# Moving four small transfers of a convolution layer from SyncE's queue to GpSimd's and ScalarE's

## The chip, the cores and the metric

The kernel runs on one core of one Trainium2 chip. The metric is the device time of one launch in microseconds (us). The kernel before took 3350.49 us, the median of three runs (3349.91 to 3353.61). A separate, profiled execution gives the durations used below.

A core has five engines, each with an instruction queue of its own that is worked through in order: PE (matrix products), DVE (VectorE), ACT (ScalarE), POOL (GpSimd) and SP (SyncE, which here only issues transfers). A transfer between the main memory and the on-chip memory is issued by one of SP, ACT or POOL and carried out by 16 DMA engines. An instruction that needs data waits for a semaphore; while it waits, nothing behind it on the same queue starts.

## What is computed

Four layers follow each other on one image of 256 x 256 pixels with 128 channels; each normalises the image by groups of channels and adds what it computes to it. The first three (an attention, and two triangle multiplications) are not touched by the change. The fourth is a convolution layer, in the reference:

```python
def c1(t):        # 3 x 3 convolution from 128 channels to one
    return conv(t, w1, SAME) + b1
def c2(t):        # 128 x 128 product at each pixel
    return einsum('bhwc,cd->bhwd', t, w2c) + b2
t = relu(c1(x))
y = concatenate([x[:, :1], x[:, 1:] + t[:, :-1]], axis=1)
u = relu(c1(y))
z_main = u + roll(y, 1, axis=1)
z = concatenate([z_main[:, :H-2], u[:, H-1:H] + y[:, H-2:H-1], y[:, H-1:H]], axis=1)
v = relu(c2(z))
p = concatenate([z[:, :, :1], z[:, :, 1:] + v[:, :, :-1]], axis=2)
r = relu(c2(p))
q_main = r + roll(p, 1, axis=2)
q = concatenate([q_main[:, :, :W-2], r[:, :, W-1:W] + p[:, :, W-2:W-1], p[:, :, W-1:W]], axis=2)
```

t and u have one channel: they are images of 256 x 256 numbers, made from the 3 x 3 convolution and added to all 128 channels.

## The kernel before

The convolution layer works on groups of 8 image rows (R = 8): 32 groups, with the 128 channels on the 128 partitions and 2048 pixels along each. The one-channel images are worked on in blocks of 16 rows (BR = 16), each spread over all 128 partitions with 33 numbers on each; there are 16 blocks, so one block belongs to two groups. The order of the instructions on each engine is the order in which the program writes them (a manual schedule), so the loop at L1695 is the order of all queues.

A block's way through the machine is this:

- `load9` (L1459) loads a group of the image x, 1 MB, eight groups ahead, from SP's queue.
- `taps` (L1464) forms, six groups ahead, the nine products of the 3 x 3 filter on PE; ACT copies them out (L1472), and SP stores them (L1477, four stores).
- `load_block` (L1494) loads them back shifted, in the block's layout (L1487).
- `sum_taps` (L1503, DVE) adds nine taps; `relu_t` (L1515, ACT) and `shift_t` (L1519 and L1522, POOL) give the block of t.
- `keep_t` (L1526) stores this block of t to the buffer tD, one row lower; `load_t` (L1529) loads the block's rows from tD, which shifts t by one image row.
- `image_u` (L1536, DVE) and `relu_u` (L1540, ACT) give u; `image_e` (L1545, POOL) adds the shifted t to u, which gives e, all that is to be added to the channels.
- `keep_e` (L1547) stores e to the buffer eD; `load_e` (L1561) loads the two groups of it as one long row each into the tile `er`, in two transfers.
- `spread_e` (L1572, POOL) copies such a row to all 128 partitions, into a tile that has one buffer.
- `start_z` (L1580, ACT) writes the scaled x into PSUM, and `finish_z` (L1595, DVE) adds the spread e: z.
- `p_half` and `q_half` (L1609, L1623, L1626 on DVE, products L1601 on PE), `residual` (L1615 to L1617, POOL) and the copy L1710 on ACT form p and q; `emit` (L1631) transposes q on PE (L1638), ACT copies it out (L1639), SP stores 1 MB (L1640).

The two-buffer PSUM pool `p9psX` is shared by `start_z`, `taps` and the transposes, in turn: two tiles of z, one of taps, two of transposes. So a transpose waits for the copy L1472 or for finish_z, and the next group's start_z waits for L1639.

For the block b = s // 2 + 2, t is made in the even group s, and u and e in the odd group that follows. In the kernel before, all of keep_t, load_t, keep_e and load_e are issued by SP, and at the head of the next group: keep_t and load_t in the odd group after load9, keep_e and load_e in the even group before load9. A load waits on SP until its store has landed. Blocks 0 to 2 are made ahead of this (`begin_image`, L1671, and `end_image`, L1678, in groups 0 and 1).

Of the kernel before, what the change touches and what calls it, by code (L numbers as in the profile page):

```python
# [16 lines left out]
P = 128  # L17
N = 256
# [14 lines left out]
def kernel(ctx: ExitStack, tc: tile.TileContext, a: dict, out: bass.AP):  # L33
    nc = tc.nc
# [33 lines left out]
    tD = dram.tile([1, (N + 2) * NP], F32, name="tD")  # L68
    eD = dram.tile([1, N * NP], F32, name="eD")
# [1031 lines left out]
    with tc.tile_pool(name="x5", bufs=7) as x5_pool, tc.tile_pool(name="p5", bufs=2) as sb, tc.tile_pool(  # L1101
# [95 lines left out]
        for s in range(NSC):  # L1197
            b, j = divmod(s, KB)
# [246 lines left out]
    NR = N // R  # L1445
    H = R // 2
    BR = 16
    NB = N // BR
    BW = NP // 8
    LEAD = 6  # L1450
    with tc.tile_pool(name="p9", bufs=2) as sb, tc.tile_pool(name="p9psM", bufs=2, space=PSUM) as psM, tc.tile_pool(
# [3 lines left out]
        xs, zs, pbs, qs, blocks = {}, {}, {}, {}, {}  # L1455
# [3 lines left out]
        def load9(s):  # L1459
            if s < NR:  # L1460
                xs[s] = sb.tile([P, R, N], F32, name="p9_x", bufs=9)
                nc.sync.dma_start(xs[s], x3r[:, s * R : (s + 1) * R, :])
# [37 lines left out]
        def image_rows(d, row, n=BR):  # L1500
            return d[:, row * NP : (row + n) * NP].rearrange("o (p w) -> p (o w)", w=BW)
# [15 lines left out]
        def shift_t(b):  # L1517
            k = blocks[b]
            nc.gpsimd.tensor_tensor(k["t"], k["t"], inside, ALU.mult)  # L1519
            t = k["t"][:, 0:BW]  # L1520
            nine = bass.AP(tensor=t.tensor, offset=t.offset, ap=[list(t.ap[0]), [1, BW], [1, TAPS]])
            nc.gpsimd.tensor_tensor(  # L1522
                k["prod"][:, :, 0:TAPS], nine, wsum.unsqueeze(1).to_broadcast([P, BW, TAPS]), ALU.mult
            )

        def keep_t(b):  # L1526
            nc.sync.dma_start(image_rows(tD, b * BR + 1), blocks[b]["t"][:, 4 : 4 + BW])

        def load_t(b):  # L1529
            t2 = blocks[b]["t2"] = sb.tile([P, BW], F32, name="p9_t2")  # L1530
            nc.sync.dma_start(t2, image_rows(tD, b * BR))

        def image_u(b):
            k = blocks[b]
# [3 lines left out]
        def relu_u(b):  # L1538
            k = blocks[b]
            nc.scalar.activation(k["u"], k["u"], AF.Relu, bias=b1)  # L1540

        def image_e(b):
            k = blocks[b]
            k["e"] = sb.tile([P, BW], F32, name="p9_e")
            nc.gpsimd.tensor_tensor(k["e"], k["u"], k["t2"], ALU.add)  # L1545

        def keep_e(b):  # L1547
            k = blocks.pop(b)
            e = k["e"]
            if b < NB - 1:  # L1550
                nc.sync.dma_start(image_rows(eD, b * BR), e)
            else:
                nc.sync.dma_start(image_rows(eD, N - BR, BR - 2), e[0 : P - 16, :])
                nc.sync.dma_start(image_rows(eD, N - 2, 1), e[P - 8 : P, :])
                nc.sync.dma_start(image_rows(eD, N - 1, 1), k["t"][P - 8 : P, 4 : 4 + BW])

        def row_e(s):
            at = 32 * (s % 4)
            return er[at : at + 1, :]

        def load_e(b):  # L1561

            for s in range(2 * b, 2 * b + 2):
                nc.sync.dma_start(
                    row_e(s).rearrange("o (h w) -> o h w", w=N),
                    eD.rearrange("o (h w) -> o h w", w=NP)[:, s * R : (s + 1) * R, 4 : 4 + N],
                )

        def spread_e(s):
            if s < NR:  # L1570
                ebs[s] = sb.tile([P, SC], F32, name="p9_eb", bufs=1)
                nc.gpsimd.partition_broadcast(ebs[s], row_e(s))  # L1572

        def start_z(s):

            zps[s] = [psX.tile([P, H, N], F32, name="p9_zp", tag="x") for _ in range(2)]

            def take(lo, hi, src):
                h = lo // H
                nc.scalar.activation(zps[s][h][:, lo - h * H : hi - h * H, :], src, AF.Identity, bias=k0, scale=r3)  # L1580

            take(0, 1, xs[s - 1][:, R - 1 : R, :] if s else xe[:, 1:2, :])
            take(1, H, xs[s][:, 0 : H - 1, :])
            if s + 1 < NR:
                take(H, R, xs[s][:, H - 1 : R - 1, :])
            else:
                take(H, R - 2, xs[s][:, H - 1 : R - 3, :])
                take(R - 2, R, xs[s][:, R - 2 : R, :])

        def finish_z(s):  # L1590
            zs[s] = sb.tile([P, R, N], F32, name="p9_z", bufs=3)
            zf, eb = zs[s].rearrange("p h w -> p (h w)"), ebs.pop(s)
            for h, zp in enumerate(zps.pop(s)):
                hs = slice(h * H2, (h + 1) * H2)
                nc.vector.tensor_tensor(zf[:, hs], zp.rearrange("p h w -> p (h w)"), eb[:, hs], ALU.add)  # L1595

        def product9(src, h):
            pm = psM.tile([P, H, N], F32, name="p9_pm")
            for c in range(2):
                r = h * H + 2 * c  # L1600
                nc.tensor.matmul(  # L1601
                    pm[:, 2 * c : 2 * c + 2, :], lhsT=w2c, rhs=src[:, r : r + 2, :], start=True, stop=True
                )
            return pm

        def p_half(s, h):
            rows_ = slice(h * H, (h + 1) * H)
            pm = product9(zs[s], h)
            nc.vector.scalar_tensor_tensor(  # L1609
                pbs[s][:, rows_, 1:N], pm[:, :, 0 : N - 1], kcol[:, 0:1], zs[s][:, rows_, 1:N], ALU.max, ALU.add  # L1610
            )
# [7 lines left out]
        def q_half(s, h):  # L1619
            rows_ = slice(h * H, (h + 1) * H)  # L1620
            q = qs[s]
            pm = product9(pbs[s], h)
            nc.vector.scalar_tensor_tensor(  # L1623
                q[:, rows_, 0 : N - 2], pm[:, :, 0 : N - 2], kcol[:, 1:2], q[:, rows_, 0 : N - 2], ALU.max, ALU.add
            )
            nc.vector.scalar_tensor_tensor(  # L1626
                q[:, rows_, N - 2 : N - 1], pm[:, :, N - 1 : N], kcol[:, 1:2], q[:, rows_, N - 2 : N - 1],
                ALU.max, ALU.add,
            )
# [41 lines left out]
        def begin_image(b):  # L1671
            sum_taps(b)
            relu_t(b)
            shift_t(b)
            keep_t(b)
            load_t(b)

        def end_image(b):  # L1678
            image_u(b)
            relu_u(b)  # L1680
            image_e(b)
            keep_e(b)
            load_e(b)
# [10 lines left out]
        spread_e(1)  # L1694
        for s in range(NR + 2):  # L1695
            b = s // 2 + 2
            if s > 3 and s % 2 == 0 and b <= NB:
                keep_e(b - 1)
                load_e(b - 1)
            load9(s + 8)  # L1700
            if s > 1 and s % 2 == 1 and b < NB:
                keep_t(b)
                load_t(b)
            if s < NR:
                pbs[s] = sb.tile([P, R, N], F32, name="p9_pb")
                nc.scalar.activation(pbs[s][:, :, 0:1], zs[s][:, :, 0:1], AF.Identity, bias=kcol[:, 0:1])
                if s + 1 < NR:
                    start_z(s + 1)
                qs[s] = sb.tile([P, R, N], F32, name="p9_q", bufs=3)
                nc.scalar.activation(qs[s], xs[s], AF.Identity, bias=kcol[:, 2:3])  # L1710
                p_half(s, 0)
                p_half(s, 1)
                del xs[s]
            if s < 2:
                begin_image(s + 1)
            if s + 1 < NR:
                finish_z(s + 1)
            if s < 2:
                end_image(s + 1)
            if 0 < s <= NR:  # L1720
                q_half(s - 1, 0)
                q_half(s - 1, 1)
                del pbs[s - 1], zs[s - 1]
            if s < NR:
                residual(s)
                spread_e(s + 2)
            if s < 2:

                for i in range(2):
                    taps(xs[4 + 2 * s + i], (4 + 2 * s + i) * R, 4)  # L1730
                load_block(s + 2)
            elif b < NB:
                sum_taps(b) if s % 2 == 0 else image_u(b)
            if s > 1 and s + LEAD < NR:
                taps(xs[s + LEAD], (s + LEAD) * R, 4)
            if s > 1 and s % 2 == 1 and b + 1 < NB:
                load_block(b + 1)
            if s > 1:
                emit(s - 2)
                if b < NB:  # L1740
                    if s % 2 == 0:
                        relu_t(b)
                        shift_t(b)
                    else:
                        relu_u(b)
                        image_e(b)
            if 0 < s <= NR:
                last = qs[s - 1][:, :, N - 1 : N]
                nc.scalar.activation(last, last, AF.Identity, bias=kcol[:, 1:2])
# [182 lines left out]
```

## Time and profile before

| what | us |
|---|---|
| median of three runs | 3350.49 |
| the profiled execution | 3354.71 |
| its span | 3353.0 |
| convolution layer, from group 0's L1710 to the end | 2960 to 3353 |
| group 2's L1710 to group 26's | 3001.08 to 3287.06 |
| L1472 (copy of the taps), each | 0.69 |
| L1710, each | 1.99 |
| L1615 (the large part of residual), each | 4.52 |
| L1572 (spread_e), each | 2.29 |
| L1639, each | 1.01 |

Engine times in the profile are those of the instruction itself. For a transfer that SP or ACT issues, the line (SPq, ACTq) is the time in which the queue was occupied with issuing it, not the transfer; when it has landed shows only in who starts next. For transfers of GpSimd the profile gives the time to landing as well. "Idle before" names what the engine waited for. L numbers are lines of the kernel before.

### The profile page before, as it was taken

To read this page: it belongs to the slowest core of one execution; us is meant where nothing else is said; L and a number is where in the kernel's file an instruction comes from. 1 tells how busy PE (TensorE), PEld (TensorE's weight loads), DVE (VectorE), ACT (ScalarE), POOL (GpSimd) and SP (SyncE) were. 2 spreads that over 40 slices of the span, in tenths; PEclk is the share of its full clock that TensorE was granted. 3 is DMA by queue.
4 is the path that set the end of the run, shared out by engine and by line. 5 is a ranking of instruction groups with operands and counts; after the bars stand their busy time and mean duration, and the time that the engine had idled before them with its cause. 6 is when DMAs were issued, how large, how long until landed. Compare 5 with 4: busy or idle time off the path is not lost. (4 is left out here: it accounts for less than half of the span.)

```text
span 3353.0 us, 51718 instructions
## 1 busy us (share of the span) xinstructions
PE 3050.1 (91%) x19780; PEld 1631.7 (49%) x19780; DVE 2243.0 (67%) x2532; ACT 2039.4 (61%) x2274; POOL 1753.9 (52%) x984
## 2 busy tenths in 40 slices
PE   5669999999999999967996999999999999749888
PEld 4515555555555555532532444444899533214444
DVE  5627888888888888863555545444555688647666
ACT  3567777777777777734586544543444477636666
POOL 4055777777777777730384000000555588546666
PEclk8889999999999999988997999999999999879999
DMA  9983333333333333359598676865999899746665
GB/s 355 370 313 94 109 120 111 111 119 109 121 107 118 108 121 109 121 209 375 171 384 343 256 270 248 305 233 216 351 350 350 319 389 384 312 137 190 194 191 148
DMA packets 298035, 749.46 MB, mean 224 GB/s; under 512 B 74679, under 2 KB 145289, under 8 KB 248601
## 3 DMA queue, kind: packets, MB, share of 16 engines
q1 hardware_dynamic: 289847, 735.49, 61.3%
q0 software_dynamic: 7648, 9.55, 0.8%
q8 instruction: 159, 2.61, 0.3%
q10 hardware_dynamic: 288, 1.05, 0.1%
q14 instruction: 93, 0.76, 0.1%
HBM read 458.34 MB, written 287.64 MB: 222 GB/s over the span
## 5 line engine op out<-in xcount | busy, mean ns | idle before, releaser
L565 DVE TENSOR_TENSOR p_e<-p_S,triT 128x1024 f32<-128x1024 f32 x512 | 609.3, 1212 | 144.2 <-PE p_S L555 144.2
L575 POOL TENSOR_TENSOR p_es<-p_e 128x1024 f32<-128x1024 f32 x256 | 603.4, 2368 | 123.8 <-issue 65.2
L573 ACT ACTIVATE p_e<-p_e,mbT 128x1024 f32<-128x1024 f32 x512 | 552.0, 1138 | 59.8 <-DVE p_e L565 59.6
L1172 PE MATMUL p_pm<-p_zn,wf 128*128 128x512 f32 x1040 | 449.3, 593 | 2.3 <-ACT p_a L1207 1.9
L540 PE MATMUL p_mm<-p_xn,w 128*128 128x512 f32 x768 | 404.6, 610 | 0.3 <-DVE p_v L535 0.3
L1172 PEld LDWEIGHTS p_pm<-p_zn,wf 128*128 128x128 f32 x1040 | 196.6, 190 | 255.1 <-issue 246.5
L555 PE MATMUL p_S<-p_q,p_k 32*128 32x256 f32 x4096 | 294.9, 400 | 3.5 <-DVE p_e L565 3.3
L1262 POOL MEMSET k<- 128x512 f32 x1 | 0.5, 520 | 505.8 <-DVE p_zn L1165 505.8
L555 PEld LDWEIGHTS p_S<-p_q,p_k 32*128 32x128 f32 x4096 | 185.7, 184 | 159.5 <-PE p_mm L531 91.7
L514 POOL TENSOR_TENSOR p_xn<-p_xn,p_rs 128x1024 f32<-128x1024 f32 x63 | 151.1, 2398 | 205.1 <-DMA p_rb<-rzD 129.1
L1890 PE MATMUL tp_z<-p_B,tp_at 128*128 128x256 f32 x1024 | 250.5, 388 | 0.7 <-DMA p_B<-bD 0.5
L588 PE MATMUL p_o<-p_e,p_v 128*32 128x256 f32 x4096 | 247.6, 382 | 0.0
L1293 POOL TENSOR_TENSOR k<-k,p_sq 128x512 f32<-128x512 f32 x128 | 163.0, 1273 | 159.1 <-ACT p_sq L1291 159.1
L1890 PEld LDWEIGHTS tp_z<-p_B,tp_at 128*128 128x128 f32 x1024 | 185.1, 191 | 23.2 <-DVE tp_at L1881 1.5
L540 PEld LDWEIGHTS p_mm<-p_xn,w 128*128 128x128 f32 x768 | 125.6, 190 | 104.2 <-issue 87.9
L1292 DVE TENSOR_TENSOR k<-tp_z,k 128x512 f32<-128x512 f32 x128 | 88.5, 692 | 126.8 <-ACT p_sq L1291 126.8
L588 PEld LDWEIGHTS p_o<-p_e,p_v 128*32 128x32 f32 x4096 | 120.0, 109 | 109.3 <-ACT p_g L546 41.5
L1289 ACT COPY p_K<-tp_z 128x512 f32<-128x512 f32 x128 | 75.1, 586 | 157.5 <-PE tp_z L1890 157.5
L546 ACT ACTIVATE p_g<-p_mm,bgh 128x512 f32<-128x512 f32 x128 | 88.0, 687 | 131.2 <-PE p_mm L540 131.2
L544 ACT ACTIVATE p_k<-p_mm,cqkg 128x512 f32<-128x512 f32 x128 | 88.1, 689 | 125.1 <-PE p_mm L540 124.9
L531 PEld LDWEIGHTS p_mm<-w,p_xn 128*128 128x128 f32 x1024 | 134.4, 191 | 61.1 <-issue 60.4
L1211 DVE SCALAR_TENSOR_TENSOR p_b<-p_pm,b2w,p_b 128x1024 f32<-128x1024 f32 x64 | 82.1, 1283 | 118.4 <-PE p_pm L1172 104.0
(374 smaller groups left out, 6092.3 us busy)
## 6 DMA issues: line engine op xcount, KB each, us to landing
p_x<-x2T SPq DMA_DIRECT2D x60, 1024.0 KB
x<-x1T SPq DMA_DIRECT2D x51, 1024.0 KB
p_x<-in_x_dram SPq DMA_DIRECT2D x32, 1024.0 KB
p_x<-xT SPq DMA_DIRECT2D x64, 512.0 KB
x2T<-x SPq DMA_DIRECT2D x32, 1024.0 KB
aD<-p_a SPq DMA_DIRECT2D x32, 1024.0 KB
bD<-p_b SPq DMA_DIRECT2D x32, 1024.0 KB
p_A<-aD SPq DMA_DIRECT2D x32, 1024.0 KB
```

The lines of the kernel that those rows point to most:

```text
L514: nc.gpsimd.tensor_tensor(xn, xn, groups[g]["rs"], ALU.mult)
L531: nc.tensor.matmul(pm[:, k * D : (k + 1) * D], lhsT=t["xn"][:, b * P : (b + 1) * P], rhs=wf[:, 2 * D : 3 * D], start=True, stop=True,)
L540: nc.tensor.matmul(pm, lhsT=w, rhs=t["xn"][:, cs_], start=True, stop=True)
L555: nc.tensor.matmul(Ss[h // 2][:, h % 2, u, :], lhsT=t["k"][hp, r * N + u * P : r * N + (u + 1) * P], rhs=t["q"][hp, r * N : (r + 1) * N], ...
L565: nc.vector.tensor_tensor(e[:, :, 2 * p : 2 * p + 2, :].rearrange("p u h n -> p h u n"), Ss[p], triT[:, 2 * p : 2 * p + 2, :, :], ALU.add,)
L573: nc.scalar.activation(e[:, u, :, :], e[:, u, :, :], AF.Exp, bias=mbT[:, u, i : i + 1])
L575: nc.gpsimd.tensor_tensor(es, e[:, 0, :, :], e[:, 1, :, :], ALU.add)
L588: nc.tensor.matmul(t["o"][hp, r % 2, :], lhsT=t["v"][:, r * 2 + u, hp], rhs=e[:, u, h, :], start=(u == 0), stop=(u == 1),)
L1172: nc.tensor.matmul(pm[:, c, :], lhsT=wf2[:, i, :], rhs=zns[s][:, k * CK : (k + 1) * CK], start=True, stop=True)
L1292: nc.vector.tensor_tensor(k1, pz, k1, ALU.add)
L1293: nc.gpsimd.tensor_tensor(k2, k2, sq, ALU.add)
L1890: nc.tensor.matmul(pz[:, t, :], lhsT=at[:, u, t * P : (t + 1) * P], rhs=Bc[:, u, :], start=(u == 0), stop=(u == 1))
```

## The change

The helpers get a parameter for the queue that issues them, with SP as default, which groups 0 and 1 keep. In the loop keep_t moves behind shift_t, and keep_e behind image_e, each on GpSimd's queue; so both are issued in the group in which the block is made. load_e (two transfers, even groups) and load_t (one, odd groups) move to ScalarE's queue, behind the copy L1710 of the group in whose head SP issued them before. In the last block keep_e is three stores. The amounts, addresses and numbers of transfers are the same.

```diff
-        def keep_t(b):
-            nc.sync.dma_start(image_rows(tD, b * BR + 1), blocks[b]["t"][:, 4 : 4 + BW])
-
-        def load_t(b):
+        def keep_t(b, queue=nc.sync):
+            queue.dma_start(image_rows(tD, b * BR + 1), blocks[b]["t"][:, 4 : 4 + BW])
+
+        def load_t(b, queue=nc.sync):
             t2 = blocks[b]["t2"] = sb.tile([P, BW], F32, name="p9_t2")
-            nc.sync.dma_start(t2, image_rows(tD, b * BR))
+            queue.dma_start(t2, image_rows(tD, b * BR))
...
-        def keep_e(b):
+        def keep_e(b, queue=nc.sync):
             k = blocks.pop(b)
             e = k["e"]
             if b < NB - 1:
-                nc.sync.dma_start(image_rows(eD, b * BR), e)
+                queue.dma_start(image_rows(eD, b * BR), e)
...
-        def load_e(b):
+        def load_e(b, queue=nc.sync):
 
             for s in range(2 * b, 2 * b + 2):
-                nc.sync.dma_start(
+                queue.dma_start(
                     row_e(s).rearrange("o (h w) -> o h w", w=N),
...
         for s in range(NR + 2):
             b = s // 2 + 2
-            if s > 3 and s % 2 == 0 and b <= NB:
-                keep_e(b - 1)
-                load_e(b - 1)
             load9(s + 8)
-            if s > 1 and s % 2 == 1 and b < NB:
-                keep_t(b)
-                load_t(b)
             if s < NR:
...
                 nc.scalar.activation(qs[s], xs[s], AF.Identity, bias=kcol[:, 2:3])
+            if s > 3 and s % 2 == 0 and b <= NB:
+                load_e(b - 1, nc.scalar)
+            if s > 1 and s % 2 == 1 and b < NB:
+                load_t(b, nc.scalar)
+            if s < NR:
                 p_half(s, 0)
                 p_half(s, 1)
...
                     if s % 2 == 0:
                         relu_t(b)
                         shift_t(b)
+                        keep_t(b, nc.gpsimd)
                     else:
                         relu_u(b)
                         image_e(b)
+                        keep_e(b, nc.gpsimd)
```

More of the change, by code (lines that the diff above doesn't have):

```diff
@@ L1550, in keep_e @@
             if b < NB - 1:
-                nc.sync.dma_start(image_rows(eD, b * BR), e)
+                queue.dma_start(image_rows(eD, b * BR), e)
             else:
-                nc.sync.dma_start(image_rows(eD, N - BR, BR - 2), e[0 : P - 16, :])
-                nc.sync.dma_start(image_rows(eD, N - 2, 1), e[P - 8 : P, :])
-                nc.sync.dma_start(image_rows(eD, N - 1, 1), k["t"][P - 8 : P, 4 : 4 + BW])
+                queue.dma_start(image_rows(eD, N - BR, BR - 2), e[0 : P - 16, :])
+                queue.dma_start(image_rows(eD, N - 2, 1), e[P - 8 : P, :])
+                queue.dma_start(image_rows(eD, N - 1, 1), k["t"][P - 8 : P, 4 : 4 + BW])
         def row_e(s):
```

## The prediction

> **What bounds the kernel now.** I read the table of 40 slices to find the last stage, then the start of each group of the convolution layer (ScalarE's L1710 runs once in each of its 32 groups), then the busy time in windows, the waits of each engine, and the timeline of one pair of groups.
>
> L1710 starts at 3023.37, 3033.14 and 3042.95 us in groups 4, 5, 6: 9.8 us a group. From group 7 on it alternates, 3078.69, 3092.82, 3102.74: 14.1 and 9.9. From group 2 (3001.08) to group 26 (3287.06) twelve pairs take 286.0 us, 23.8 a pair, where two undisturbed groups take 19.6. The columns below are the window, its length, each engine's busy time (and instructions), PE clock, DMA share and GB/s:
> ```profile
> 3000.00:3050.00 50.00, 48.66 (x200) 23.77 (x199) 40.83 (x47) 36.75 (x46) 40.21 (x27) 1.00 0.64 179
> 3150.00:3200.00 50.00, 43.58 (x164) 21.64 (x163) 34.98 (x40) 32.33 (x43) 31.26 (x22) 0.93 0.69 198
> ```
> In the first window PE is full (48.7 of 50); in the second nothing is, so a latency bounds it. The waits of POOL, DVE, PE and SP between 3000 and 3290 us (total, times, longest) name it:
> ```profile
> POOL p_eb L1572 <- DMA p_er<-eD: 47.1, 9, 6.5
> POOL p_e L1545 <- DMA p_t<-tD: 21.8, 8, 3.0
> DVE p_z L1595 <- POOL p_eb L1572: 42.0, 12, 5.2
> PE p_pp L1468 <- DVE p_z L1595: 30.8, 11, 3.9
> SPq L1531 <- DMA tD<-p_t: 62.0, 12, 5.9
> SPq L1564 <- DMA eD<-p_e: 29.5, 11, 3.5
> ```
> PE waits for z, z for the spread e, the spread for e's rows from memory. The timeline of POOL and of SP's queue closes the ring:
> ```profile
> 3080.55 2.29 POOL L1572 PARTITION_BROADCAST p_eb<-p_er  x1 [4.66 <-DMA p_er<-eD]
> 3082.92 0.27 POOL L1519 TENSOR_TENSOR p_t<-p_t,p_in 128x41 f32<-128x41 f32 x1
> 3083.27 0.81 POOL L1522 TENSOR_TENSOR p_prod<-p_t,wsum 128x297 f32<-128x297 f32 x1
> ...
> 3094.13 0.26 POOL L1545 TENSOR_TENSOR p_e<-p_u,p_t 128x33 f32<-128x33 f32 x1 [2.84 <-DMA p_t<-tD]
> ...
> 3104.68 2.29 POOL L1572 PARTITION_BROADCAST p_eb<-p_er  x1 [4.91 <-DMA p_er<-eD]
> ```
> ```profile
> 3082.11 3.86 SPq L1462 DMA_DIRECT2D p_x<-x3T  x1
> 3086.06 0.42 SPq L1527 DMA_DIRECT2D tD<-p_t  x1
> 3092.31 0.32 SPq L1531 DMA_DIRECT2D p_t<-tD  x1
> ...
> 3096.51 0.98 SPq L1640 DMA_DIRECT2D out_dram<-p_o  x1
> 3097.59 2.56 SPq L1551 DMA_DIRECT2D eD<-p_e  x1
> 3102.48 1.27 SPq L1564 DMA_DIRECT2D p_er<-eD  x2
> ```
> Read down: spread and shift_t to 3084.08 (3.53); SP still issues an image load, so the store of t starts 1.98 later; it lands and the load is let go at 3092.31 (6.25); t is back at 3094.13 (1.82); e made (0.26); SP reaches its store 3.20 later; landed at 3102.48 (4.89); rows loaded by 3104.68 (2.20). Sum 24.13, the whole period. POOL, DVE and PE only follow.
>
> [...] a store behind large transfers on SP's queue needs 4.9 to 6.3 us. [...] after a PE gap of 2.85 us the window 3084 to 3086 has clock 0.50, and the tap products take 1.93 instead of 1.07 us, the transposes 2.54 instead of 1.97: 1.4 us.
>
> **The change, part by part**, in microseconds per pair (even group E, odd group O); st is the start of ScalarE's L1472 of a group.
>
> *SP.* It loses five issues and the two waits on stores (62.0 + 29.5 us above). SP is not on the path otherwise; its gain is that output stores and image loads are issued up to a group earlier: 3096.51 above stores what ScalarE had ready at 3089.65. Worth nothing in itself, but it moves the 2 MB of each group to just behind the copies of L1639.
>
> *POOL, keep_t and keep_e.* Two issues a pair. GpSimd's stores to triD (rows below) cost 0.51 each, so 1.0 a pair. POOL's work is then 2 x (4.9 + 2.4) + 1.2 + 0.3 + 1.0 = 17.1, under 19.6: free as long as 2.5 of slack remain. The 1.98 and 3.20 of SP's lateness vanish.
>
> *The landing, called L*, from the start of POOL's issue to release. This is the unknown. GpSimd's stores to triD in the first layer (min/median/max in ns, then us) bound it:
> ```profile
> L424 POOL DMA_DIRECT2D triD<-p_tr x93: 502/508/538, 163.7 to 243.5; - x93
> DMA to landing us min/median/max: 1.8/6.0/8.0
> ```
> Asked window by window: 1.8 with the DMA engines nearly idle (share 0.05), 3.0 at 0.11, 3.9 at 0.60, 5.0 to 6.5 at 0.8 to 1.0, at most 8.0. A store of t starts (below) 6.9 after st of E, and the group's 2 MB, at 334 to 393 GB/s over some 5.7 us, are sent from about 3.5 to 10 after st: in the middle. The store of e comes at about 4 after a delayed st of O, at the start of the next burst. I take L = 4.8 for both, between 3.9 and 5.5; ends 1.8 and 8.0.
>
> *ACT, load_t and load_e.* They stand behind L1710 and in front of L1472, L1639, relu and start_z of the next group. Each waits for its store, and ACT's queue waits with it. Issue costs 0.32 for t and 1.27 for the two rows of e (SP's rows). The pause of ACT between L1710 and L1472 is 1.69, so the cover is thin. When the loads are let go:
> - L1710 of E ends 1.69 before st(E). residual 4.89 and 0.07 of gap, spread 2.29 + 0.1, shift_t 1.17 + 0.1 follow on POOL: store of t at st(E) + 6.9. st(O) is free at 6.9 + L + 0.32 = 12.0, instead of 9.8. So ACT, and with it the second half of the transposes on PE (it needs L1472's buffer), stand for 2.2.
> - relu_u comes 3.3 after st(O), image_e then, so the store of e at 15.8; the load is done at 15.8 + 4.8 + 1.3 = 21.9. Without this wait the next st(E) comes 9.8 after st(O), at 21.8: covered.
> - PE's gap of 2.2 is shorter than the 2.85 that halved the clock: I add 0.6, between 0 and 1.4.
>
> Period: 6.9 + 4.8 + 0.32 + 9.8 + 0.6 = 22.4. A second ring, L1472 to the end of the next L1710 (8.1) and then POOL's 8.5, gives 16.6 + 4.8 + 0.4 = 21.8: below it. Rows of e arrive 0.93 after their issue, before residual of E ends, so the 4.9 of POOL's wait is gone.
>
> *Order.* The instruction lists of both kernels show nothing else moved: the stores stand right behind L1522 and L1545 on POOL, the loads right behind L1710 on ACT; PE and DVE are as before.
>
> **Sum.** Twelve pairs: 286.0 - 12 x 22.4 = 17 saved. Groups 26 to 28 run at 18.4 the pair, with no tap products; the last load waits there cost about 1. Gain 16. The profiled execution took 3354.7 (span 3353.0 and 1.7 around it) and would take 3338.7; the median of the runs is 4.2 lower, 3350.5, so the time is 3334.
>
> **Rivals.**
> - *Fast: [...].* L about 3.0, as at light load. Period 6.9 + 3.0 + 0.3 + 9.8 = 20.0 (PE again sets it at 19.6 if L is under 2.6). 12 x 3.8 = 46 less 1: 3306. [...] Against: triD's landings [...] needed 5 to 6.5 in busy stretches. Chance 0.28.
> - *Nothing:* L of 5.5 to 6.1 gives 23.4 to 24.3, against 23.8 now: 3350. Chance 0.10.
> - *Slower: ACT stands behind its own load.* The place is the load of t in front of L1472. At L = 6.8, as in the worst busy stretches, st(O) comes at 14.0, PE idles 4.2 and pays the clock's 1.3: 25.1 a pair, 15 lost, 1 at the end: 3366. It decides from L = 5.9 (6.9 + 5.9 + 0.3 + 9.8 + 1.0 = 23.9). Against: DMA share in these windows is 0.62 to 0.70, with lulls of 0.1 to 0.2. Chance 0.25.
> - *The change does not do what it says:* excluded by the lists.
>
> **Chances.** Forecast 0.37, fast 0.28, nothing 0.10, slower 0.25. About 0.2% (6.7 us) is what a measurement of this kernel can tell from no change. Faster 0.65, same 0.10, slower 0.25. Range 3306 to 3362: L from 3.0 to about 6.5, with less than a tenth left out on each side. The forecast alone: L 3.6 to 5.5, 3314 to 3345.
>
> **What would show it.** Right: POOL's wait for eD's rows falls from 47 to a few us; ACT waits in front of L1472 for DMA tD<-p_t about 2 a pair; L1710 spacing near 12 then 10; GpSimd's stores 0.5 each and landing in 4 to 5.5. Wrong: no wait of ACT on tD, and groups at 9.8 (the fast rival); or PE idle over 4 in odd groups with clock 0.50 (the slow one); or a new wait elsewhere, for instance POOL late by more than its slack of 2.5, or image_e waiting for t again.

## The result, and the profile after

The changed kernel takes 3345.54 us (median of 10 runs, 3340.94 to 3349.4). In the same comparison the kernel before took 3355.23 (10 runs, 3349.91 to 3359.84). The ratio is 0.997, with an interval of 0.996 to 0.998: 9.7 us less. The forecast was 16 us less than the profiled execution of the kernel before, and a time of 3334. The profiled execution of the changed kernel took 3345.7 (span 3342.8). The copy into q, L1710 before, is L1704 now; the lines up to L1640 have kept their numbers.

The waits of ScalarE, of PE and of POOL between 2990 and 3280 us (total, times, longest) are these:
```profile
ACT p_st L1472 <- DMA tD<-p_t: 42.7, 11, 4.7
ACT p_st L1472 <- PE p_pp L1468: 30.4, 15, 3.4
```
```profile
PE p_pt L1638 <- ACT p_st L1472: 22.2, 11, 2.8
```
```profile
POOL p_q L1615 <- ACT p_q L1704: 48.9, 22, 3.8
...
POOL p_eb L1572 <- DMA p_er<-eD: 0.7, 1, 0.7
```
POOL's wait for the rows of e, 47.1 before, is all but gone. In its place stands ScalarE, in front of L1472, until the store of t has landed: 11 times, 3.9 each. Of each 3.9 about 1.7 is the pause that ScalarE has there in an undisturbed group (the other waits at L1472, 30.4 in 15, are 2.0 each); the other 2.2 are the price of issuing the load from ScalarE. PE hands the wait on: its second half of the transposes waits 22.2 / 11 = 2.0 for L1472. POOL now waits for ScalarE (48.9), as a follower.

The tile views of tD and of eD give GpSimd's stores and the time to landing:
```profile
L1527 POOL DMA_DIRECT2D tD<-p_t x13: 555/555/582, 3018.7 to 3285.3; - x13
...
DMA to landing us min/median/max: 2.3/5.0/6.1
```
```profile
L1551 POOL DMA_DIRECT2D eD<-p_e x12: 555/555/577, 3029.9 to 3275.2; - x12
...
DMA to landing us min/median/max: 1.5/3.0/4.4
```
One pair of groups on the timeline shows the new ring, the cycle of waits that sets the period. The columns are start, duration, engine, line, operation, and in brackets the idle time before it with its cause:
```profile
3058.25 0.69 ACT L1472 ACTIVATE p_st<-p_pp,s 128x512 f32<-128x512 f32 x1 [1.73 <-PE p_pp L1468]
...
3064.83 0.56 POOL L1527 DMA_DIRECT2D tD<-p_t  x1
...
3069.88 0.32 ACTq L1531 DMA_DIRECT2D p_t<-tD  x1
3070.38 0.69 ACT L1472 ACTIVATE p_st<-p_pp,s 128x512 f32<-128x512 f32 x1 [4.04 <-DMA tD<-p_t]
...
3071.12 1.09 PE L1638 MATMUL p_pt<-ident,p_q 128*128 128x128 f32 x8 [2.14 <-ACT p_st L1472]
...
3074.31 0.56 POOL L1551 DMA_DIRECT2D eD<-p_e  x1 [0.29 <-POOL p_e L1545]
...
3077.35 1.95 ACTq L1564 DMA_DIRECT2D p_er<-eD  x2
...
3080.15 0.69 ACT L1472 ACTIVATE p_st<-p_pp,s 128x512 f32<-128x512 f32 x1 [1.73 <-PE p_pp L1468]
```
Read down from L1472 of the even group: the store of t 6.58 later, landed and the load issued 5.05 after that, L1472 of the odd group 12.13 after the first, the next even one 9.77 on. The pair takes 21.9. Twelve pairs, from group 2's copy into q to group 26's, take 267.55 (285.98 before): 22.3 a pair.

### The profile page after: what moved, and what is told of

Same layout as the page of the kernel before. It is cut to its first block, busy times and chain, and to the rows that moved or that the text cites. A ratio compares the mean times of both kernels' runs of the same rounds, so it can differ in the third digit from the quotient of the medians.

```text
span 3342.8 us, 51721 instructions
## 1 busy us (share of the span) xinstructions
PE 3049.3 (91%) x19780; PEld 1630.5 (49%) x19780; DVE 2241.1 (67%) x2532; ACT 2038.4 (61%) x2274; POOL 1769.9 (53%) x1012
## 5 line engine op out<-in xcount | busy, mean ns | idle before, releaser
L1615 POOL TENSOR_TENSOR p_q<-p_q,p_pb 128x2024 f32<-128x2024 f32 x32 | 144.1, 4504 | 64.8 <-ACT p_q L1704 52.8
```

Source lines behind the costliest of these rows:

```text
L1615: nc.gpsimd.tensor_tensor(q[:, :, 1 : N - 2], q[:, :, 1 : N - 2], pb[:, :, 0 : N - 3], ALU.add)
```

## The experiments

The theory: in every pair ScalarE's queue is held by its own load of t, for as long as the store needs to land, and this sets the period. Rival one: the wait for e's rows, or POOL's own work, still sets it, and ScalarE only follows. Rival two: the time is one of loaded DMA engines, and who issues a transfer doesn't matter. The table has the medians and, from one profile each, the layer (group 0's copy into q to the end) and the mean of the twelve pairs from group 2's copy into q to group 26's.

| kernel | median us (runs) | ratio to before | layer | pair |
|---|---|---|---|---|
| before, first profile | 3355.23 (10) | 1 | 392.7 | 23.83 |
| after, first profile | 3345.54 (10) | 0.997 [0.996, 0.998] | 375.5 | 22.30 |
| n1_before | 3353.94 (12) | 1.0002 [0.9994, 1.0011] | 391.9 | 23.92 |
| n2_after | 3341.19 (5) | 0.9964 [0.995, 0.9978] | 378.2 | 22.61 |
| e3_loads_sp | 3323.60 (4) | 0.9918 [0.9901, 0.9934] | 363.4 | 21.42 |
| e4_load_t_late | 3346.53 (8) | 0.9976 [0.9965, 0.9987] | 387.8 | 23.42 |
| e5_stores_sp | 3367.87 (5) | 1.0042 [1.0028, 1.0056] | 406.0 | 24.89 |
| e6_no_out | 3335.90 (4) | 0.995 [0.9933, 0.9966] | 375.0 | 22.46 |
| e7_loads_first | 3320.14 (4) | 0.9902 [0.9886, 0.9919] | 359.7 | 21.14 |
| e8_both_late | 3326.96 (4) | 0.9919 [0.9903, 0.9936] | 362.1 | 21.24 |

The kernel before took 3353.92 beside the first four experiments and 3353.93 beside the last four.

### n1_before and n2_after: both kernels again

No edit. The first profile after had the layer begin 7 us later than the one before (2967.31 against 2960.34), which no part of the change explains.

> The kernel before, unchanged, profiled again beside the others of this call. What is asked: whether the stages ahead of the convolution layer take the same time in each profile. In the first two profiles the convolution layer (from its first L1710 or L1704 to the end) took 392.7 us before and 375.5 after, 17.2 less, but its first L1710 came 7.0 us later in the profile after, so the spans differ by 10.2 only. Theory (the change touches the layer alone; the 7 us are from chip to chip and run to run): ahead of the layer this profile and the one of the changed kernel in this call agree within 2 us, the layer takes 391 to 394, and the changed kernel is 15 to 18 us faster than this one here. Rival (the change costs something ahead of the layer): the first L1710 at 2960 here and 2967 for the changed kernel again.

> The changed kernel, unchanged, profiled again on the same chip as the kernel before. Theory: the layer takes 374 to 377 us, 22.3 us for a pair of groups, the first L1704 comes where the first L1710 of the kernel before does within 2 us, and the kernel is 15 to 18 us faster. Rival: the first L1704 comes 7 us later than the other's L1710, and 10 us are gained.

The layer began at 2963.74 in n1_before and at 2960.98 in n2_after: the 7 us did not come again, so they belong to that execution (a shift of an us or two is not excluded by two profiles each). The layer's saving shows again, 391.9 - 378.2 = 13.7, and on average 392.3 - 376.9 = 15.4. Timed, it is 3353.92 - 3341.19 = 12.7 here and 9.7 in the first comparison, less than the 15 to 18 expected.

The waits are not quite those of the first profile: ScalarE stood for t in 8 odd groups here, 31.9 us in all between 2990 and 3290, and once for the load of e:
```profile
3051.99 1.28 ACTq L1564 DMA_DIRECT2D p_er<-eD  x2
3053.48 0.69 ACT L1472 ACTIVATE p_st<-p_pp,s 128x512 f32<-128x512 f32 x1 [5.45 <-issue]
```
In the odd group ahead of it, t had held next to nothing: its L1472 waited 1.94, for PE. The step from group 6 to group 7 took 14.4 in place of 9.8. e4 and e6 come back to this.

### e3_loads_sp: the loads back on SyncE, the stores left with GpSimd

```diff
-                load_e(b - 1, nc.scalar)
+                load_e(b - 1)
...
-                load_t(b, nc.scalar)
+                load_t(b)
```

> The stores stay on GpSimd, the loads of t and e go back to SP's queue, at the same place in the program (behind load9). Theory, that what is left over the 19.6 us of PE for a pair is ScalarE standing in front of L1472 behind its own load: the wait of L1472 for tD is gone, groups of 9.8 to 10.2, a pair 19.6 to 20.4 instead of 22.3, and the kernel is 22 to 32 us faster than the changed kernel, about 40 faster than the one before. Rival, that the landing of GpSimd's store itself sets the period, whoever waits for it: a pair stays at 22 to 22.5 and the time within 4 us of the changed kernel. A third: SP stands instead, and its stores of taps and output come late; then DVE waits for L1487, and a pair is 21 to 24.

Both loads stand behind load9 here, where the kernel before had load_e ahead of it; e7 has them ahead. Measured 3323.6: 30 us under the kernel before and 17.6 under n2_after, less than the 22 to 32 expected, at 21.4 a pair for 19.6 to 20.4. From group 4 on most steps from group to group are 9.8, which is PE's pace, with single ones of 10.5 to 16.6. The waits of ScalarE, SyncE's queue and POOL between 2995 and 3280 us:
```profile
ACT p_st L1472 <- PE p_pp L1468: 59.2, 25, 7.0
```
```profile
SPq L1531 <- DMA tD<-p_t: 75.9, 13, 6.8
```
```profile
POOL p_eb L1572 <- DMA p_er<-eD: 31.1, 11, 6.2
```
ScalarE has no wait on tD left. The wait has moved to SyncE's queue (75.9 in 13), where little that is urgent stands behind it: the third outcome, DVE waiting for the loads of taps (L1487), comes to 1.0 us in all between 2990 and 3290. So the theory's wait was real and on the path, and rival two falls: the same transfers, with the same stores, are worth 17.6 us more or less by who waits for them. What remains above 19.6 is, in the main, POOL's wait for rows, a part of rival one: between 3010 and 3270 us DVE waits 20.3 us for the spread (10 times), and PE 13.2 us for DVE's z (6 times).

### e4_load_t_late: only the load of t moved back on ScalarE

`load_t` is taken from behind the copy into q and put behind `emit` in the odd group, ahead of `relu_u`. Behind it stand only relu_u and the next group.
```diff
-            if s > 1 and s % 2 == 1 and b < NB:
-                load_t(b, nc.scalar)
...
                     else:
+                        load_t(b, nc.scalar)
                         relu_u(b)
```

> As the changed kernel, but the load of t stands on ScalarE's queue behind the two copies L1639 of its group instead of in front of L1472. Theory: the store of t (6.9 us after L1472 of the even group, 5 to land) has landed by 11.9, and the load is reached at 9.8 + 2.9 = 12.7, so ScalarE does not stand any more: the 2.2 us a pair are gone, unless the store of e (3 to 4.5 to land) now holds the even group. A pair 19.7 to 21.2 instead of 22.3; 12 to 30 us faster than the changed kernel. Rival, that the period is bounded by the landings in a ring (store, load, store, load): a pair stays at 22.

A miss: 3346.53, no better than after. (The profile fell on the slowest of the eight runs, 3350.13, so its 23.4 a pair is rather too high.) L1472 is held by t no more, and yet it is held. ScalarE's waits between 2995 and 3280 us, and one pair on the timeline:
```profile
ACT p_st L1472 <- issue: 47.1, 10, 5.5
```
```profile
3069.46 0.56 POOL L1551 DMA_DIRECT2D eD<-p_e  x1 [0.29 <-POOL p_e L1545]
...
3075.00 1.26 ACTq L1564 DMA_DIRECT2D p_er<-eD  x2
3076.38 0.69 ACT L1472 ACTIVATE p_st<-p_pp,s 128x512 f32<-128x512 f32 x1 [4.57 <-issue]
```
Now the load of e is let go 5.54 after the start of its store (3069.46 to 3075.00; the median in this stretch is 5.4, in place of 3.0), and this load of two rows, the other load on ScalarE, holds L1472 in the even groups. The expectation's "unless" is what happened. "issue" in the first line is that load: the profile names nothing waited for, but the line above it shows ScalarE's queue busy with it until 3076.26. Two things have changed for e. POOL starts its store 10.0 after the copy into q of the odd group in both profiles, but in the changed kernel the wait for t holds back L1472 of the odd group, and with it the next group: from the store of e to the time at which the next L1472 is due, 9.77 after that of the odd group, there are 5.84 there and 4.04 here. That is 1.8 of cover lost. And the landing takes 2.5 longer; why is not shown (the DMA engines are full in the 3 us from the store's start in both, with a share of 1.03 and 1.12 at the median). So the second load takes the place of the first, at nearly the same price (47.1 in 10 for 42.7 in 11).

### e5_stores_sp: the other half alone, stores on SyncE and loads on ScalarE

```diff
+            if s > 3 and s % 2 == 0 and b <= NB:
+                keep_e(b - 1)
             load9(s + 8)
+            if s > 1 and s % 2 == 1 and b < NB:
+                keep_t(b)
...
-                        keep_t(b, nc.gpsimd)
...
-                        keep_e(b, nc.gpsimd)
```

> The other half alone: the loads stay on ScalarE as in the changed kernel, the stores of t and e go back to SP, to the head of the next group where they were (the store of e before load9, that of t behind it). Theory, that the store's own queue is what shortened the ring (5.0 us to land for t and 3.0 for e on GpSimd's queue, against 6.3 and 4.9 behind SP's large transfers, plus 2.0 and 3.2 of lateness of SP): now ScalarE stands for the late store as well, the load of t is let go some 13 to 16 us after L1472 of the even group, and a pair takes 24 to 27 us. The kernel is 10 to 40 us slower than the changed kernel, and slower than the one before. Rival, that moving the loads off SP was what gained: a pair of 21 to 22.5, as fast as the changed kernel.

Slower than before by 14 us: 24.9 a pair. ScalarE's waits between 3000 and 3270 us:
```profile
ACT p_st L1472 <- DMA tD<-p_t: 28.7, 7, 5.3
ACT p_st L1472 <- issue: 28.4, 6, 5.0
```
Both loads now hold ScalarE, t's in odd and e's in even groups ("issue" as in e4), since the stores are issued late, behind SyncE's large transfers: in one group e is ready at 3073.05, its store is issued at 3074.34 and takes 2.40 to issue, and the rows are let go at 3080.01, 7.0 after e was ready. Moving the stores alone thus gave -30 (e3), moving the loads alone +14 (e5). The two don't simply add up: -16 would be their sum, and both together gave -8.4 to -12.7 (3345.54 and 3341.19 against 3353.93). With the stores on GpSimd, the loads on ScalarE cost 17.6 to 22 (against e3).

### e6_no_out: lighter DMA traffic

The changed kernel, leaving out the output stores of groups 2 to 27.
```diff
-            nc.sync.dma_start(
+            if s < 2 or s > 27:
+                nc.sync.dma_start(
```

> The changed kernel with the output stores of groups 2 to 27 left out (26 MB of output are not written), so that the DMA engines have half the load in the layer. Theory, that the 5.0 us a store of t needs to land are the load on the shared DMA engines: landing of t falls to 2 to 3.5 us, ScalarE no longer stands in front of L1472 for longer than its 1.7, and a pair takes 19.6 to 20.5; 20 to 33 us faster than the changed kernel. Rival, that 5 us are what GpSimd's way of storing takes: landing 4.5 to 5 and a pair at 22.

Two windows of the changed kernel, and the same two of this one (columns as in the prediction; DMA share is the last but one):
```profile
3050.00:3100.00 50.00, 45.66 (x174) 21.79 (x173) 35.19 (x40) 36.79 (x49) 36.24 (x29) 0.97 0.74 208
3100.00:3150.00 50.00, 46.42 (x195) 22.79 (x194) 40.09 (x47) 34.15 (x46) 38.18 (x29) 1.00 0.76 225
```
```profile
3050.00:3100.00 50.00, 46.31 (x172) 22.68 (x171) 34.62 (x40) 35.20 (x48) 36.11 (x30) 0.94 0.44 129
3100.00:3150.00 50.00, 43.93 (x161) 21.82 (x160) 33.23 (x39) 32.18 (x41) 33.44 (x26) 0.90 0.38 107
```
The store of t then lands in 2.3 instead of 5.0 (medians; this one between 3000 and 3270 us), as rival two would have it, and ScalarE waits for tD once. The pair does not follow, at 22.46 where 19.6 to 20.5 were expected, nor does the layer, 375.0 for 375.5 and 378.2. (The time of 3335.9 is 5 to 10 lower than the changed kernel's, not the 20 to 33 expected; in the profile the layer began early, at 2956.16. Where the 5 to 10 come from is not shown.) ScalarE's waits between 3000 and 3270 us say why the pair stays:
```profile
ACT p_st L1472 <- issue: 27.3, 6, 5.4
...
ACT p_st L1472 <- DMA tD<-p_t: 3.7, 1, 3.7
```
As in e4, the load of e holds L1472 once t doesn't: its store lands in 4.4. The means above hide why. In the 3 us from the start of each store the DMA share (medians, between 3000 and 3270 us) was 0.43 for t here, for 0.99 in the changed kernel; for e it was 1.09 even here. So in these two kernels the landing of t went with the share at that moment, 5.0 at 0.99 and 2.3 at 0.43, and e's was 4.4 at 1.09; the shorter landing of t alone bought little, at 22.46 a pair.

### e7_loads_first: loads on SyncE, at the head of the group

As e3, with load_e and load_t ahead of load9 in place of behind the copy into q:
```diff
+            if s > 3 and s % 2 == 0 and b <= NB:
+                load_e(b - 1)
+            if s > 1 and s % 2 == 1 and b < NB:
+                load_t(b)
             load9(s + 8)
...
-                load_e(b - 1, nc.scalar)
...
-                load_t(b, nc.scalar)
```

> Stores on GpSimd; loads of t and e on SP, but ahead of load9 in their group instead of behind it. With the loads behind load9 the spread of e still waited 31.1 us in all for its rows (11 times, at most 6.2), and groups of 13 to 16 us were left among those of 9.8. Theory, that the 1 MB of load9 in front, in SP's order and in the DMA engines, is what delays the rows: the wait falls under 10 us, a pair takes 19.7 to 20.6, and the kernel is 8 to 20 us faster than with the loads behind load9, near 3308 to 3315. Rival, that load9 then comes late or SP's wait holds the stores of taps back: a pair of 21 to 23, with DVE or PE waiting for L1487's or L1462's tiles.

3320.14, the lowest of all. It is not told apart from e3 (their intervals overlap), and the 8 to 20 expected over e3 did not come. The landing of e is 2.0 at the median, and its store falls into a lull (DMA share 0.29 in the 3 us from its start), but the rows are late all the same. SyncE's queue and POOL around one even group:
```profile
3100.05 0.56 POOL L1551 DMA_DIRECT2D eD<-p_e  x1 [0.29 <-POOL p_e L1545]
...
3103.16 1.97 SPq L1640 DMA_DIRECT2D out_dram<-p_o  x1
3105.23 3.07 SPq L1564 DMA_DIRECT2D p_er<-eD  x2
...
3110.30 2.30 POOL L1572 PARTITION_BROADCAST p_eb<-p_er  x1 [4.10 <-DMA p_er<-eD]
```
SyncE reaches the load only after the output store, 5.2 behind the store of e, and its issue takes 3.07, where two rows are issued in 1.26 elsewhere. POOL's wait for these rows (24.6 in 9 between 3000 and 3270 us) is the largest that is left over PE's pace, 21.1 against 19.6; that it is all of the difference is not shown.

### e8_both_late: both loads on ScalarE, where nothing urgent stands behind them

e4, and in even groups load_e and the spread of its row moved behind `emit` as well:
```diff
-            if s > 3 and s % 2 == 0 and b <= NB:
-                load_e(b - 1, nc.scalar)
...
-                spread_e(s + 2)
+                late = s > 3 and s % 2 == 0 and b <= NB
+                if not late:
+                    spread_e(s + 2)
...
                 emit(s - 2)
+                if s < NR and late:
+                    load_e(b - 1, nc.scalar)
+                    spread_e(s + 2)
```

> Both loads on ScalarE, but behind the copies L1639 of their groups (spread_e of even groups is then written behind the load; GpSimd's order stays). With the load of t alone moved, the wait of ScalarE went to the load of e: 4.5 us before L1472 of even groups. Theory, that ScalarE in front of L1472 is the place where it hurts: no group waits there any more, rows of e come some 2 us later than residual ends, which GpSimd's slack of 2.5 a pair covers; a pair 19.7 to 21; 15 to 30 us faster than the changed kernel. Rival, that the ring of landings takes over: a pair of 21.5 to 23, with GpSimd waiting for the rows of e or for t.

3326.96, 27 us under the kernel before with both loads on ScalarE, and 14 to 19 under the changed kernel. ScalarE's waits in front of L1472, and POOL's for rows, between 3000 and 3270 us:
```profile
ACT p_st L1472 <- PE p_pp L1468: 43.5, 23, 3.0
```
```profile
POOL p_eb L1572 <- DMA p_er<-eD: 22.7, 7, 5.5
```
No load holds L1472. So it is not ScalarE's queue that costs, but the place in it: in front of a copy for which PE waits. POOL's wait for rows is back, as in e3, and the pair is 21.2, a little over the 19.7 to 21 expected.

## Why the prediction was wrong in size

The direction, the mechanism and the period held, and the time lies in the range. The forecast's 3334 is 11.5 too low, and what failed are two terms of its last sum. The base of 3350.5 was too low: that is 4.7 of the 11.5. And the gain in the layer was counted whole as time gained: 16.5 between 3350.5 and 3334, where 9.7 were timed; that is the other 6.8. Point by point:

- *The old ring of waits.* Right. With GpSimd's stores its waits went (POOL for rows 47.1 to 0.7), and e3 shows the gain without the new wait.
- *POOL, two issues.* 0.56 each for 0.51. POOL had the slack. Right.
- *The landing L.* For t 5.0 for the 4.8 taken: right. For e 3.0 for 4.8: wrong, on the harmless side, since the load of e was covered.
- *ScalarE held in front of L1472.* 2.2 forecast, 3.9 - 1.7 = 2.2 measured, and PE behind it, 2.0. The store of t at 6.58 (6.9), L1472 of the odd group at 12.13 (12.0), the store of e at 16.06 (15.8), the next even group 9.77 on (9.8).
- *The load of e, costed at nothing.* Covered, in all pairs of the first profile and in all but one of n2_after. In the pair shown, its issue ended 21.05 after L1472 of the even group, and L1472 came at 21.9. But the margin was 0.9, and in the forecast there was none (done at 21.9, due at 21.8 without that wait); it came from two errors that offset each other in part, a landing of 3.0 for 4.8 and an issue of 1.95 for 1.27. What the text should have said is that a part of the cover is the wait for t itself: it holds back the odd group while e goes on. e4 and e6 took that away and met the load of e, whose store then landed in 5.4 and 4.4.
- *The clock.* 0.6 a pair taken for the pause of PE, by its length. PE's second half of the transposes waited in 11 odd groups, 1.75 to 2.83 each. After four of these gaps, of 1.75 to 2.20, the granted clock was 0.50 for 3.41 us; after the other seven, the longest among them, it stayed at full speed:
```profile
3093.07 1.09 PE L1638 MATMUL p_pt<-ident,p_q 128*128 128x128 f32 x8 [2.20 <-ACT p_st L1472]
3094.00 5.29 PE L1601 MATMUL p_pm<-p_z,w2c 128*128 128x512 f32 x8
...
3160.42 1.09 PE L1638 MATMUL p_pt<-ident,p_q 128*128 128x128 f32 x8 [2.83 <-ACT p_st L1472]
3161.35 3.60 PE L1601 MATMUL p_pm<-p_z,w2c 128*128 128x512 f32 x8
```
  After the four, ScalarE's next L1472 had to wait 0.8 to 1.7 longer for PE: 5.2 in all, 0.4 a pair, which is what the pair of 22.3 has over the 21.9 of the ring. So the mean came near 0.6, but the length of the gap does not decide it, as the forecast supposed.
- *The period.* 22.4 forecast, 22.3 and 22.6 measured. Right. The gain is not spread evenly: the pair of groups 4 to 6, at 19.6 before, takes 22.4 after, because before the ring had first to use up its lead, and after ScalarE is held from the start.
- *The end.* From group 26 on 65.9 before (65.94 and 65.74) and 67.7 after (67.78 and 67.70): 1.9 lost for the 1 forecast.
- *The sum.* The layer saved 15.4 on average in two profiles each, for 16. This is right. That all of it would show in the time is the second step that failed: the timed gain is 9.7 and 12.7. In the first two profiles the layer saved 17.2, but it began 7.0 later, and 1.2 more lay outside the span (2.9 for 1.7), which leaves 9.0 between the two executions.
- *The base: the first step that failed.* "The median of the runs is 4.2 lower, 3350.5, so the time is 3334." Three runs were a low draw: with seven more the median is 3355.23, and in two later comparisons it is 3353.92 and 3353.93. The profiled execution's own 3354.7 was the better base, and would have given 3338.7.
- *What is left.* From 3338.7 to 3341.2 or 3345.5, 2.5 to 6.8. The tail's 0.9 is a part. Over all 15 timed runs of after and 38 of before (n1_before's twelve not among them) the medians are 3343.8 and 3354.0, a gain of 10.2; the profiled executions gave 3356.8 (3354.71 and 3358.79) and 3343.4 (3345.7 and 3341.19), a difference of 13.3. So of the 5.2 between the layer's 15.4 and the timed 10.2, 2.8 is that the profiles of before fell, on average, on slower executions than its median, and 2.1 is the start of the layer, which moves by some us from profile to profile in kernels that differ only behind it (2956 to 2967 in ten of them). Why it moves is open, and that this is the cause of the rest is argued, not shown: two profiles don't give the mean execution of either kernel.

The rivals: the fast one needed L near 3, and for t L was 5.0. Its price of 20.0 a pair left out the load of e: in e6, with 2.3 for t but 4.4 for e, the pair still took 22.46. No run had about 3 for both with the loads in this place, so the price itself stays open. The slow one, ScalarE behind its own load, had the mechanism right, and its threshold of 5.9 wasn't reached at the median. With the stores on SyncE (e5) ScalarE did stand that long, at 24.9 a pair for its 25.1; but there the load of e held it too, so the likeness of the numbers is luck. "Nothing" needed L over 5.5.

That the store of t would land sooner on a queue other than SyncE's was the author's estimate. On GpSimd's it landed in 5.0 at the median of the changed kernel, where before its load was let go 6.05 after the start of SyncE's store (13 stores between 2990 and 3290 us, at most 6.6). With a DMA share of 0.43 and 0.35 in the 3 us from its start, in e6 and e8, it landed in 2.3 and 2.0. No run sets the queue apart from the moment of the store, so what each of the two is worth is not shown.

## What to carry to other kernels

Moving a transfer to another queue moved its wait too (for the store of t 62.0 us on SyncE's queue before, 42.7 in front of ScalarE's L1472 after, 75.9 on SyncE's queue in e3): before choosing the queue, list what stands behind the waiting load and who waits for that. A step "covered" by another wait is only as safe as that wait: price it once more with that wait gone, or the next improvement will stop at it (47.1 us in front of L1472 in e4 and 27.3 in e6, for the load of e). And a forecast of half a per cent needs a base of more than three runs, and an idea of how far a gain in one stage shows in the whole.

## What the runs showed that was not expected

- The same store of t, 0.56 to issue on GpSimd, landed in 5.0, 2.3 or 2.0 us (medians of the changed kernel, e6 and e8), where the DMA share in the 3 us from its start was 0.99, 0.43 and 0.35. e8 stores all of the output, and its mean share is 0.71 to 0.79 in windows of 50 us (0.71 to 0.76 in the changed kernel): the landing followed the share at the moment of the store, not the mean. With busy engines the share does not settle it: stores of e landed in 3.0 at 1.03 (changed kernel) and in 5.4 at 1.12 (e4).
- The issue of the same two rows occupied a queue for 1.26 to 2.06 us on ScalarE, for 1.3 on SyncE in the kernel before, and for 3.07 to 3.95 on SyncE in e7 (between 3040 and 3160 us), right behind the issue of a 1 MB store.
- PE's clock fell after four gaps of 1.75 to 2.20 us and not after one of 2.83 (products of up to 5.29 in place of 3.60). After each of the four it stayed at 0.50 for 3.41.
